# A graph network's edge weights: three BF16 one-hot products replaced by one FP32 product

## The chip, the cores and the metric

The kernel runs on one core of a Trainium2 chip. The metric is device time in microseconds. The time before is the median of three runs.

## The reference

The program is a stack of four graph layers over 3125 nodes with 128 features and 100000 edges, sorted by destination. All four layers use the same edges, so two dense matrices serve them: for each pair of nodes the number of edges between them, and the sum of their edge weights. Only layer 1 reads the second one:

```python
def spmv(v):
    return jax.ops.segment_sum(edge_vals[:, None] * v[edge_col], edge_row, num_segments=n)
...
x = x + _L0_gnn_ref(h, edge_index, ...)              # attention, two rounds: counts
x = x + _L1_gnn_ref(h, edge_weight, weights, src, dst)   # spmv three times: weights
x = x + _L2_gnn_ref(h, src, dst, ...)                # mean over neighbours, three rounds: counts
x = x + _L3_gnn_ref(h, edge_index, edge_type_16, ...)    # messages with edge types
```

## The kernel before

**Nodes, blocks and slots.** The nodes form 25 blocks of 128. A bucket holds the edges from one source block to one destination block; it has a fixed number of slots of 128 edges each. That number, `CAP`, depends on the destination block: 8, 4, 3, 3 for blocks 0 to 3, 2 for blocks 4 to 18 and 1 for blocks 19 to 24. Destination block 0 so has 200 slots, block 1 has 100, blocks 2 and 3 have 76, those with `CAP` 2 have 50 and those with `CAP` 1 have 26.

**Placing the edges (`place_edges`).** Vector, scalar and tensor engine compute the row of each edge in a DRAM table and pack a record of eight BF16 fields per edge into the SBUF tile `rec`: source lane, destination lane, the weight as three BF16 parts whose sum is the FP32 weight (`split3`, lines 919 to 921), and the edge type. Each field is transposed on TensorE (line 1074) and copied from PSUM into `rec` by ScalarE (line 1075). Then 782 indirect DMAs, issued one after the other by GpSimd (POOL, line 1081), scatter 128 records each into the table; each record's row is 64 bytes. The order of these DMAs (`ORDER`) puts the edges of destination blocks 5 to 24 first.

**Building a block (`build_block`).** When the records of a destination block have landed, SyncE loads them (line 1151, one slot to a partition). TensorE transposes every field into the PSUM tile `keys` (line 1157), so that one edge lies on one partition. The slots are then taken in batches of eight. For a batch, VectorE writes two one-hots of 128 x 1024 BF16, `oh_s` and `oh_d` (line 1174), and then `oh_s` times each weight part, three times, into `oh_w` (line 1176). For each slot TensorE computes the counts, `oh_s` by `oh_d` (line 1188), and then three products of `oh_d` with the parts of `oh_w` (line 1191), all in BF16, accumulated over the slots of a bucket in the PSUM tile `ps_cw`. That tile holds two source blocks and has two buffers. ScalarE copies it out: the counts as FP8 into SBUF (line 1195), the weights as FP32 into `w_out` (line 1196), which goes to DRAM from ScalarE's DMA queue (line 1199). At a block's end ScalarE sums the excess of its counts over 15 (line 1201), for a check whose result chooses a general path at the end. The one-hot tiles have two buffers each.

**Order.** `graph_and_layer0` takes the destination blocks in groups: 5 to 8, 9 to 12, 13 to 16, 17 to 20, 21 to 24, then 0 to 2, then 3 and 4. After the blocks of a group have been built, `attend` runs the first attention round for them: per block 25 matmuls with the counts (`ps_u`, line 1331), some of them taken during the build, and then for each of four heads 25 VectorE operations (line 1340), each followed by up to four matmuls (line 1343). The framework's scheduler orders the instructions of each engine when the program is built[...].

Of the kernel before, what the change touches and what calls it, by code (L numbers as in the profile page):

```python
# [18 lines left out]
P = 128  # L19
N = 3125  # L20
NB = 25
# [36 lines left out]
FIELDS = 8  # L58
# [2 lines left out]
ORDER = list(range(LOW[FIRST], ROWS)) + list(range(LOW[FIRST]))  # L61
GROUPS = [(q, q + 4) for q in range(FIRST, NB, 4)] + [(0, 3), (3, 5)]
BATCH = 8
SL, DL, WT, TYPE = 0, 1, 2, 5
CB = [(q, min(4, NB - q)) for q in range(0, NB, 4)]


def bc(ap, shape):
    return ap.to_broadcast(shape)
# [829 lines left out]
class FastGnn(Gnn):  # L899
# [24 lines left out]
    def place_edges(self, placed):  # L924


        nc, tc, a = self.nc, self.tc, self.a
        self.table = self.dram.tile([TABLE, ROOM], BF16, name="table")
        self.types = self.dram.tile([1, EPART * EC], BF16, name="types")
        self.src_of = self.dram.tile([P, EPART, EK], I32, name="src_of")  # L930
        self.dst_of = self.dram.tile([P, EPART, EK], F32, name="dst_of")
# [2 lines left out]
        with ExitStack() as s:  # L934
# [4 lines left out]
            tile = lambda name, dt=F32: work.tile([A, EC], dt, name=name)  # L939


            rec = placed.tile([P, EK * A * FIELDS + ROOM - FIELDS], BF16, name="rec")
            rec_of = rec[:, : EK * A * FIELDS].rearrange("p (k a f) -> p k a f", k=EK, f=FIELDS)
            whole = E // EC
            rest = E - whole * EC
# [3 lines left out]
            for name, dt, fill, skip, queue in loads:  # L949
# [2 lines left out]
                v = a[name[:3] if skip else name]  # L952
                queue.dma_start(t[:whole, :], v[skip : skip + whole * EC].rearrange("(p c) -> p c", c=EC))
                queue.dma_start(t[whole:, : rest - skip], v[whole * EC + skip :][None, :])
            nc.gpsimd.memset(rec, 0.0)
            per = BASE[NB] // P
            none = work.tile([P, 14 * ROOM], BF16, name="none")
            nc.gpsimd.memset(none, -1.0)
            nc.sync.dma_start(self.table[: BASE[NB]].rearrange("(p i r) f -> p i (r f)", p=P, r=14),
                              bc(none[:, None, :], [P, per // 14, 14 * ROOM]))  # L960
            number = tile("number")
            nc.gpsimd.iota(number, pattern=[[1, EC]], base=0, channel_multiplier=EC, allow_small_or_imprecise_dtypes=True)

# [155 lines left out]
    def open_build(self, s, counts):  # L1119
        nc, tc = self.nc, self.tc  # L1120
        self.counts = counts.tile([P, NB, NP], FP8, name="counts8")
        self.weights = self.dram.tile([NB, P, NP], F32, name="weights")
        self.wide = self.dram.tile([2, sum(N_SLOTS[:WIDE]) * P], BF16, name="wide")
        one = self.b_one = s.enter_context(tc.tile_pool(name="build", bufs=1))
        self.b_slots = s.enter_context(tc.tile_pool(name="build_s", bufs=1))
        self.b_hot = s.enter_context(tc.tile_pool(name="build_hot", bufs=2))
        self.b_out = s.enter_context(tc.tile_pool(name="build_out", bufs=3))
        self.b_ps = s.enter_context(tc.tile_pool(name="build_ps", bufs=2, space=PSUM))
        self.b_keys = s.enter_context(tc.tile_pool(name="build_keys", bufs=1, space=PSUM))
        self.lane16 = one.tile([P, P, 2], BF16, name="lane16")  # L1130
        nc.vector.tensor_copy(self.lane16, bc(self.lane[:, :, None], [P, P, 2]))
        self.minus_most = one.tile([P, 1], F32, name="minus_most")
        nc.vector.memset(self.minus_most, -MOST)
        self.above = one.tile([P, NB], F32, name="above")
        self.junk = one.tile([P, NB, P], FP8, name="junk")

    def build_block(self, db):
        nc, tc = self.nc, self.tc
        lane = self.lane16
        cap = CAP[db]  # L1140
        n_slots = N_SLOTS[db]
        halves = -(-n_slots // P)
        rows = n_slots // halves
        need = [self.placed[c] for c in range(LOW[db], ENDS[db])]


        keys = self.b_keys.tile([P, WT + 3, N_SLOTS[0]], BF16, name="keys")
        at = sum(N_SLOTS[:db])
        for a in range(halves):
            r = self.b_slots.tile([P, P, ROOM], BF16, name="slots")  # L1150
            ld = nc.sync.dma_start(r[:rows], self.table[BASE[db] + a * rows * P :][: rows * P].rearrange(
                "(s e) f -> s e f", e=P))
            for ins in need:
                self.wait_for(ld.ins, ins)
            tc.declare_no_dep(ld.ins, group=self.table.tensor.name, keep=need, reason="its edges are in these")
            for f in range(WT + 3):
                nc.tensor.transpose(keys[:, f, a * rows : (a + 1) * rows], r[:rows, :, f], self.ident16[:rows, :rows])
            if db < WIDE:
                rowed = self.b_one.tile([P, 2, P], BF16, name="rowed")
                for i, f in enumerate((SL, TYPE)):  # L1160
                    nc.scalar.copy(rowed[:rows, i], r[:rows, :, f])  # L1161
                    nc.scalar.dma_start(self.wide[i, (at + a * rows) * P : (at + (a + 1) * rows) * P].rearrange(
                        "(s e) -> s e", e=P), rowed[:rows, i])
        if db < WIDE:
            nc.scalar.copy(self.wide_dl[:, at : at + n_slots], keys[:, DL, :n_slots])
        for x0 in range(0, n_slots, BATCH):
            k = min(BATCH, n_slots - x0)
            h = k // 2
            wide = [P, h, P, 2]
            key = lambda f: bc(keys[:, f, x0 : x0 + 2 * h].rearrange("p (a b) -> p a b", b=2)[:, :, None, :], wide)  # L1170
            oh_s, oh_d = (self.b_hot.tile([P, BATCH // 2, P, 2], BF16, name=m) for m in ("oh_s", "oh_d"))
            oh_w = self.b_hot.tile([P, 3, BATCH // 2, P, 2], BF16, name="oh_w")
            for oh, f in ((oh_s, SL), (oh_d, DL)):
                nc.vector.tensor_tensor(oh[:, :h], bc(lane[:, None], wide), key(f), op=OP.is_equal)  # L1174
            for t in range(3):
                nc.vector.tensor_tensor(oh_w[:, t, :h], oh_s[:, :h], key(WT + t), op=OP.mult)  # L1176
            for x in range(k):
                sb, c = divmod(x0 + x, cap)
                if sb == NB:
                    break  # L1180
                i, j = divmod(sb, 2)
                if j == c == 0:
                    ps = self.b_ps.tile([P, 2, 2, P], F32, name="ps_cw")
                if c == 0 and sb % 4 == 0:
                    w_out = self.b_out.tile([P, 4, P], F32, name="w_out")
                of = (slice(None), x // 2, slice(None), x % 2)
                last = c == cap - 1
                nc.tensor.matmul(ps[:, 0, j, :], lhsT=oh_s[of], rhs=oh_d[of], start=(j == c == 0), stop=last,  # L1188
                                 skip_group_check=True)
                for t in range(3):  # L1190
                    nc.tensor.matmul(ps[:, 1, j, :], lhsT=oh_d[of], rhs=oh_w[:, t][of], start=False,  # L1191
                                     stop=(last and t == 2), skip_group_check=True)
                if last and (j == 1 or sb == NB - 1):
                    q, n = 2 * i, j + 1
                    nc.scalar.copy(self.counts[:, q : q + n, db * P : (db + 1) * P], ps[:, 0, :n], saturate=True)  # L1195
                    nc.scalar.copy(w_out[:, q % 4 : q % 4 + n], ps[:, 1, :n])
                    if sb % 4 == 3 or sb == NB - 1:
                        b = sb // 4 * 4
                        nc.scalar.dma_start(self.weights[db, :, b * P : (sb + 1) * P].rearrange("p (b s) -> p b s", s=P),
                                            w_out[:, : sb + 1 - b])  # L1200
        nc.scalar.activation(self.junk, self.counts[:, :, db * P : (db + 1) * P], AF.Relu, bias=self.minus_most,
                             accum_out=self.above[:, db : db + 1], saturate=False)

    def load_graph(self, dst, b, weights=False):
        self.nc.sync.dma_start(dst.rearrange("p b s -> p (b s)"), self.weights[b])
# [705 lines left out]
```

## Time and profile before

| | us |
|---|---|
| Median of the runs | 4530.33 (4530.28 to 4541.58) |
| Profiled execution, its own time | 4554.83 |
| Its span | 4553.0 |
| First and last scatter DMA start (line 1081) | 140.3 and 1207.5 |
| First and last one-hot of the build start (line 1174) | 490.6 and 2225.6 |
| Mean granted TensorE clock | 0.874 |

The profile is of one execution, taken on the chip. Engines are named PE (TensorE matmuls), PEld (its weight loads), DVE (VectorE), ACT (ScalarE), POOL (GpSimd) and SP (SyncE). A row of the groups gives the line of the code, the engine, the operation, the tile written and those read, the shape of one, how many there were, and behind the bar their busy time, the mean of one in ns, and the time for which the engine stood idle just ahead of them with what ended most of it. "remote" stands for a release by something that the profile does not show. A matmul's time in it overlaps with that of the next, so that the distance between two starts tells more than the duration of one. A busy share is an average over stages with different limits.

### The profile page before, as it was taken

How to read it: one execution, taken by the hardware profiler on the slowest of the kernel's cores; microseconds unless marked ns; L12 is line 12 of the kernel's file. 1: busy time of each engine (PE TensorE's matmuls, PEld its weight loads, DVE VectorE, ACT ScalarE, POOL GpSimd, SP SyncE). 2: the span in 40 equal slices, each digit the busy share in tenths (PEclk: the TensorE clock that was granted, in tenths of full speed). 3: DMA queues.
4: the chain of work that ended last, by engine and by line, in shares of the span. 5: the costliest groups of instructions: out<-in, count | busy, mean ns of one | idle time of the engine just before them, and what ended most of it. 6: DMA issues, size and time to landing. Idle time of an engine off the chain costs nothing.

```text
span 4553.0 us, 51360 instructions
## 1 busy us (share of the span) xinstructions
PE 2715.6 (60%) x20811; PEld 1890.9 (42%) x20811; DVE 2399.1 (53%) x3942; ACT 673.3 (15%) x1437; POOL 1277.9 (28%) x1234
## 2 busy tenths in 40 slices
PE   0010000000188878778878885988979994777777
PEld 0010000000156555555545553444455554666666
DVE  8510200000199999899989997011145563444445
ACT  0200100000024313412220001000021111222222
POOL 0577777777400000000000000000012104555553
PEclk9999955555599999999999998999989996888888
DMA  4000000000012101201000001866600003333332
GB/s 131 17 7 6 16 8 8 8 8 12 19 40 73 55 31 55 86 21 40 30 15 1 1 1 60 303 246 235 240 18 1 1 12 99 94 90 98 89 85 68
DMA packets 116937, 276.49 MB, mean 61 GB/s; under 512 B 27445, under 2 KB 67268, under 8 KB 105732
## 3 DMA queue, kind: packets, MB, share of 16 engines
q1 hardware_dynamic: 52182, 198.30, 12.9%
q0 software_dynamic: 37856, 32.76, 3.2%
q10 hardware_dynamic: 26652, 42.05, 2.5%
q8 instruction: 165, 2.70, 0.2%
q14 instruction: 82, 0.67, 0.0%
HBM read 210.00 MB, written 63.02 MB: 60 GB/s over the span
## 4 chain that ended last, share of the span: by engine, by line
PE 33%; DVE 28%; another core or an unknown queue 23%; issue 10%; ACT 4%; DMA 1%; POOL 1%; ACTq 0%; SPq 0%; DVEq 0%; POOLq 0%
DVE over L1340 10%; PE ps_sum L531 9%; DVE oh_w L1176 5%; PE ps_acc L1343 5%; PE agg_wide L1771 3%; PE agg_far L1810 3%; PE ps_agg L1601 3%; PE ps_acc L1331 2%; DVE oh_s L1174 2%; DVE oh_d L1174 2%; PE ps_m L1764 2%; PE ps_cw L1191 1%; PE ps_u L1331 1%; ACT m_wide L1768 1%
## 5 line engine op out<-in xcount | busy, mean ns | idle before, releaser
L1081 POOL DMA_INDIRECT table<-rec,idx x782 | 819.8, 1048 | 379.1 <-issue 248.5
L1343 PE MATMUL ps_acc<-parts,over 128*128 128x198 bf16 x5000 | 622.6, 252 | 166.3 <-DVE over L1340 80.0
L1633 POOL IOTA of_i<- 96x1 int32 x1 | 0.1, 131 | 2119.6 <-PE ps L510 2119.6
L1188 PE MATMUL ps_cw<-oh_d,oh_s 128*128 128x128 bf16 x1350 | 304.7, 228 | 433.2 <-remote 304.4
L1343 PEld LDWEIGHTS <-over 128*128 128x128 bf16 x5000 | 371.5, 98 | 415.3 <-DVE over L1340 392.5
L1789 POOL DMA_INDIRECT m_far<-pre,src x401 | 396.5, 989 | 473.6 <-issue 261.8
L1174 DVE TENSOR_TENSOR oh_s<-lane,keys 128x1024 bf16<-128x1024 bf16 (+2 forms) x187 | 118.3, 633 | 711.5 <-remote 669.7
L1191 PE MATMUL ps_cw<-oh_w,oh_d 128*128 128x128 bf16 x4050 | 400.6, 229 | 94.4 <-DVE oh_w L1176 48.9
L1340 DVE SCALAR_TENSOR_TENSOR over<-ps_row,minus,counts 128x512 bf16<-128x512 f32 (+2 forms) x700 | 424.5, 685 | 4.1 <-ACT rowed L1161 2.2
L531 PE MATMUL ps_sum<-g,v_node 128*128 128x512 f32 (+1 forms) x1050 | 403.7, 547 | 2.2 <-ACT v_node L482 1.4
L1340 DVE SCALAR_TENSOR_TENSOR over<-row,minus,counts 128x640 bf16<-128x640 f32 x500 | 402.0, 878 | 0.6 <-ACT row L1439 0.6
L1191 PEld LDWEIGHTS <-oh_d 128*128 128x128 bf16 x4050 | 313.1, 102 | 133.9 <-issue 112.9
L1188 PEld LDWEIGHTS <-oh_s 128*128 128x128 bf16 x1350 | 136.3, 101 | 464.8 <-issue 401.7
L1176 DVE TENSOR_TENSOR oh_w<-oh_s,keys 128x1024 bf16<-128x1024 bf16 (+2 forms) x561 | 324.9, 631 | 0.0
L1601 PE MATMUL ps_agg<-l_parts,counts 128*128 128x384 bf16 (+1 forms) x1875 | 315.9, 327 | 8.8 <-POOL l_parts L921 8.8
L1331 PE MATMUL ps_u<-parts,counts 128*128 128x396 bf16 x625 | 152.4, 356 | 281.8 <-issue 239.1
L1771 PE MATMUL agg_wide<-m_wide,oh_wide 128*128 128x128 f32 x1100 | 187.8, 322 | 168.2 <-ACT m_wide L1768 105.1
L531 PEld LDWEIGHTS ps_sum<-g,v_node 128*128 128x128 f32 x1050 | 188.0, 190 | 218.0 <-issue 215.2
L1195 ACT ACTIVATE counts<-ps_cw 128x256 fp8e4<-128x256 f32 (+1 forms) x325 | 122.5, 377 | 1021.5 <-remote 731.4
L1331 PEld LDWEIGHTS <-counts 128*128 128x128 fp8e4 x1250 | 112.8, 99 | 384.4 <-issue 302.3
L1601 PEld LDWEIGHTS <-counts 128*128 128x128 fp8e4 x1875 | 183.4, 98 | 133.6 <-issue 10.2
L1771 PEld LDWEIGHTS agg_wide<-m_wide,oh_wide 128*128 128x128 f32 x1100 | 160.7, 224 | 188.0 <-ACT m_wide L1768 122.2
(348 smaller groups left out, 3428.6 us busy)
## 6 DMA issues: line engine op xcount, KB each, us to landing
g<-weights SPq DMA_DIRECT2D x75, 1600.0 KB
weights<-w_out ACTq DMA_DIRECT2D x150, 256.0 KB
src_row<-wide SPq DMA_DIRECT2D x32, 512.0 KB
table<-rec,idx POOLq DMA_INDIRECT x782
type_row<-wide SPq DMA_DIRECT2D x32, 384.0 KB
table<-none SPq DMA_DIRECT2D x1, 10864.0 KB
type_row<-types SPq DMA_DIRECT2D x25, 384.0 KB
m_far<-pre,src POOLq DMA_INDIRECT x401
```

Of the source, the lines that this page charges most:

```text
L531: nc.tensor.matmul(ps[:, c, :w], lhsT=y[:, b, :], rhs=flat[:, c0 : c0 + w], start=(b == 0), stop=(b == NB - 1))
L1081: st = nc.gpsimd.indirect_dma_start(out=self.table, out_offset=bass.IndirectOffsetOnAxis(ap=idx[:, k, p : p + 1], axis=0), in_=rec[:, (k * ...
L1174: nc.vector.tensor_tensor(oh[:, :h], bc(lane[:, None], wide), key(f), op=OP.is_equal)
L1176: nc.vector.tensor_tensor(oh_w[:, t, :h], oh_s[:, :h], key(WT + t), op=OP.mult)
L1188: nc.tensor.matmul(ps[:, 0, j, :], lhsT=oh_s[of], rhs=oh_d[of], start=(j == c == 0), stop=last, skip_group_check=True)
L1191: nc.tensor.matmul(ps[:, 1, j, :], lhsT=oh_d[of], rhs=oh_w[:, t][of], start=False, stop=(last and t == 2), skip_group_check=True)
L1331: nc.tensor.matmul(wide[:, : HEADS * 3 * F1], lhsT=self.counts[:, sb, (a + q) * P : (a + q + 1) * P], rhs=parts[:, sb, :, :, F1:], start=( ...
L1340: V.scalar_tensor_tensor(over[:, : n * P], row, minus[:, sb, i : i + 1], self.counts[:, sb, cols], op0=OP.is_gt, op1=OP.mult)
L1343: nc.tensor.matmul(ps[:, j, : 3 * F2], lhsT=over[:, j * P : (j + 1) * P], rhs=parts[:, sb, i].rearrange("p s f -> p (s f)"), start=(sb == ...
L1601: nc.tensor.matmul(ps[:, :n], lhsT=self.counts[:, sb, db * P : (db + 1) * P], rhs=parts[:, sb, :n], start=(sb == 0), stop=(sb == NB - 1))
L1771: nc.tensor.matmul(agg, lhsT=oh[:, j, :], rhs=m[:, j, :], start=(x == 0), stop=(x == n_slots - 1))
L1789: nc.gpsimd.indirect_dma_start(out=m[:, j, :], out_offset=None, in_=pre, in_offset=bass.IndirectOffsetOnAxis(ap=src_of[:, a + j : a + j + ...
```

## The change

The weight stays one FP32 number. The record keeps its eight 16-bit places; places 2 and 3 hold the FP32 weight, and the edge type moves to place 4. The tile `rec` and the table are declared as 32-bit integers, with the same bytes. In place of three split parts, the raw weight is transposed in FP32 and copied into the record. In the build, one FP32 one-hot `oh_w` (`oh_s` times the FP32 weight) stands for the three BF16 ones, with its elements in order as before; ScalarE copies `oh_d` to FP32 (`oh_d32`), and one FP32 product per slot replaces the three BF16 products. The transposed fields of a block are two in BF16 and one in FP32. The sum over a block's counts is taken in five parts of five source blocks each.

```diff
-SL, DL, WT, TYPE = 0, 1, 2, 5
+SL, DL, WT, TYPE = 0, 1, 2, 4
...
-        self.table = self.dram.tile([TABLE, ROOM], BF16, name="table")
+        self.table = self.dram.tile([TABLE, ROOM // 2], I32, name="table")
...
-            rec = placed.tile([P, EK * A * FIELDS + ROOM - FIELDS], BF16, name="rec")
+            words = placed.tile([P, (EK * A * FIELDS + ROOM - FIELDS) // 2], I32, name="rec")
+            rec = words.bitcast(BF16)
+            rec_w = words[:, : EK * A * FIELDS // 2].bitcast(F32).rearrange("p (k a f) -> p k a f", k=EK, f=FIELDS // 2)
...
-            nc.gpsimd.memset(rec, 0.0)
+            nc.gpsimd.memset(words, 0)
...
-                              bc(none[:, None, :], [P, per // 14, 14 * ROOM]))
+                              bc(none.bitcast(I32)[:, None, :], [P, per // 14, 14 * ROOM // 2]))
...
-            parts = [tile(f"w16_{i}", BF16) for i in range(3)]
-            self.split3(parts, w, tile("rest"), V)
+            for q, n in ((0, 4), (4, EK - 4)):
+                ps = psum2.tile([P, 4, A], F32, name="ps_idx")
+                for j in range(n):
+                    nc.tensor.transpose(ps[:, j, :], w[:, (q + j) * P : (q + j + 1) * P], self.ident[:A, :A])
+                nc.scalar.copy(rec_w[:, q : q + n, :, WT // 2], ps[:, :n])
             of_i = tile("of_i", I32)
-            fields = [(WT + i, p) for i, p in enumerate(parts)]
+            fields = []
...
-                    in_=rec[:, (k * A + p) * FIELDS :][:, :ROOM], in_offset=None)
+                    in_=words[:, (k * A + p) * FIELDS // 2 :][:, : ROOM // 2], in_offset=None)
...
-        self.above = one.tile([P, NB], F32, name="above")
-        self.junk = one.tile([P, NB, P], FP8, name="junk")
+        self.above = one.tile([P, NB * 5], F32, name="above")
+        self.junk = one.tile([P, 5, P], FP8, name="junk")
...
-        keys = self.b_keys.tile([P, WT + 3, N_SLOTS[0]], BF16, name="keys")
+        both = self.b_keys.tile([P, 2, N_SLOTS[0]], F32, name="keys")
+        keys = both[:, 0].bitcast(BF16).rearrange("p (f x) -> p f x", f=2)
+        w_of = both[:, 1]
...
-            for f in range(WT + 3):
-                nc.tensor.transpose(keys[:, f, a * rows : (a + 1) * rows], r[:rows, :, f], self.ident16[:rows, :rows])
+            part = slice(a * rows, (a + 1) * rows)
+            for f in (SL, DL):
+                nc.tensor.transpose(keys[:, f, part], r[:rows, :, f], self.ident16[:rows, :rows])
+            nc.tensor.transpose(w_of[:, part], whole.bitcast(F32)[:rows, :, WT // 2], self.ident[:rows, :rows])
...
-            oh_w = self.b_hot.tile([P, 3, BATCH // 2, P, 2], BF16, name="oh_w")
+            oh_w, oh_d32 = (self.b_hot.tile([P, BATCH // 2, P, 2], F32, name=m) for m in ("oh_w", "oh_d32"))
             for oh, f in ((oh_s, SL), (oh_d, DL)):
-                nc.vector.tensor_tensor(oh[:, :h], bc(lane[:, None], wide), key(f), op=OP.is_equal)
-            for t in range(3):
-                nc.vector.tensor_tensor(oh_w[:, t, :h], oh_s[:, :h], key(WT + t), op=OP.mult)
+                nc.vector.tensor_tensor(oh[:, :h], bc(lane[:, None], wide), key(keys[:, f]), op=OP.is_equal)
+            nc.vector.tensor_tensor(oh_w[:, :h], oh_s[:, :h], key(w_of), op=OP.mult)
+            nc.scalar.copy(oh_d32[:, :h], oh_d[:, :h])
...
-                for t in range(3):
-                    nc.tensor.matmul(ps[:, 1, j, :], lhsT=oh_d[of], rhs=oh_w[:, t][of], start=False,
-                                     stop=(last and t == 2), skip_group_check=True)
+                nc.tensor.matmul(ps[:, 1, j, :], lhsT=oh_d32[of], rhs=oh_w[of], start=False, stop=last,
+                                 skip_group_check=True)
...
-        nc.scalar.activation(self.junk, self.counts[:, :, db * P : (db + 1) * P], AF.Relu, bias=self.minus_most,
-                             accum_out=self.above[:, db : db + 1], saturate=False)
+        for q in range(0, NB, 5):
+            nc.scalar.activation(self.junk, self.counts[:, q : q + 5, db * P : (db + 1) * P], AF.Relu, bias=self.minus_most,
+                                 accum_out=self.above[:, db * 5 + q // 5 : db * 5 + q // 5 + 1], saturate=False)
```

More of the change, by code (lines that the diff above doesn't have):

```diff
@@ L1144, in build_block @@
         need = [self.placed[c] for c in range(LOW[db], ENDS[db])]
-        keys = self.b_keys.tile([P, WT + 3, N_SLOTS[0]], BF16, name="keys")
+        both = self.b_keys.tile([P, 2, N_SLOTS[0]], F32, name="keys")
+        keys = both[:, 0].bitcast(BF16).rearrange("p (f x) -> p f x", f=2)
+        w_of = both[:, 1]
         at = sum(N_SLOTS[:db])
         for a in range(halves):
-            r = self.b_slots.tile([P, P, ROOM], BF16, name="slots")
-            ld = nc.sync.dma_start(r[:rows], self.table[BASE[db] + a * rows * P :][: rows * P].rearrange(
+            whole = self.b_slots.tile([P, P, ROOM // 2], I32, name="slots")
+            r = whole.rearrange("p e f -> p (e f)").bitcast(BF16).rearrange("p (e f) -> p e f", f=ROOM)
+            ld = nc.sync.dma_start(whole[:rows], self.table[BASE[db] + a * rows * P :][: rows * P].rearrange(
                 "(s e) f -> s e f", e=P))
@@ L1169, in build_block @@
             wide = [P, h, P, 2]
-            key = lambda f: bc(keys[:, f, x0 : x0 + 2 * h].rearrange("p (a b) -> p a b", b=2)[:, :, None, :], wide)
+            key = lambda v: bc(v[:, x0 : x0 + 2 * h].rearrange("p (a b) -> p a b", b=2)[:, :, None, :], wide)
             oh_s, oh_d = (self.b_hot.tile([P, BATCH // 2, P, 2], BF16, name=m) for m in ("oh_s", "oh_d"))
-            oh_w = self.b_hot.tile([P, 3, BATCH // 2, P, 2], BF16, name="oh_w")
+            oh_w, oh_d32 = (self.b_hot.tile([P, BATCH // 2, P, 2], F32, name=m) for m in ("oh_w", "oh_d32"))
             for oh, f in ((oh_s, SL), (oh_d, DL)):
-                nc.vector.tensor_tensor(oh[:, :h], bc(lane[:, None], wide), key(f), op=OP.is_equal)
-            for t in range(3):
-                nc.vector.tensor_tensor(oh_w[:, t, :h], oh_s[:, :h], key(WT + t), op=OP.mult)
+                nc.vector.tensor_tensor(oh[:, :h], bc(lane[:, None], wide), key(keys[:, f]), op=OP.is_equal)
+            nc.vector.tensor_tensor(oh_w[:, :h], oh_s[:, :h], key(w_of), op=OP.mult)
+            nc.scalar.copy(oh_d32[:, :h], oh_d[:, :h])
             for x in range(k):
```

## The prediction

> **What bounds the kernel now.** I read four views in this order: the page's engine totals and slices, the instruction groups, the timeline of the graph build, and a table of busy time by stretch. The page first (engine, busy us, share, instructions), then the groups that the change touches:
>
> ```profile
> PE 2715.6 (60%) x20811; PEld 1890.9 (42%) x20811; DVE 2399.1 (53%) x3942; ACT 673.3 (15%) x1437; POOL 1277.9 (28%) x1234
> ...
> L1188 PE MATMUL ps_cw<-oh_d,oh_s 128*128 128x128 bf16 x1350 | 304.7, 228 | 433.2 <-remote 304.4
> ...
> L1191 PE MATMUL ps_cw<-oh_w,oh_d 128*128 128x128 bf16 x4050 | 400.6, 229 | 94.4 <-DVE oh_w L1176 48.9
> ...
> L1176 DVE TENSOR_TENSOR oh_w<-oh_s,keys 128x1024 bf16<-128x1024 bf16 (+2 forms) x561 | 324.9, 631 | 0.0
> ```
>
> No engine is full over the whole span, so the build has to be read by stage. It has two. Until 1236 us POOL scatters edges and the build crawls; the timeline of VectorE there (start, duration, instruction, idle before it):
>
> ```profile
> 558.09 0.69 DVE L1174 TENSOR_TENSOR oh_s<-lane,keys 128x1024 bf16<-128x1024 bf16 x1 [61.39 <-remote]
> 566.49 0.69 DVE L1174 TENSOR_TENSOR oh_d<-lane,keys 128x1024 bf16<-128x1024 bf16 x1 [7.71 <-remote]
> ...
> 656.11 0.69 DVE L1174 TENSOR_TENSOR oh_s<-lane,keys 128x1024 bf16<-128x1024 bf16 x1 [87.15 <-remote]
> ```
>
> With two buffers, oh_s of batch three waits for the last L1188 of batch one and oh_d for the last L1191, three matmuls later on PE: 8.40 us apart, 2.8 us a matmul. That gap returns at 664.51, 768.14, 869.00, 969.82 and 1210.77. From one batch to the next it is 100.8 us (869.00 to 969.82), that is 36 matmuls of 2.8 us: 32 of the eight slots and some four of L1331. So here PE's matmul completions are rationed, whatever their length. FP32 counts double: the two L1258 copies at 393.45 and 404.65 us stand 11.20 us apart, with two FP32 products between, which the trace records as four MATMULs.
>
> After 1236 us the build runs freely, in turns with the attention. Busy time by stretch (stretch, length, then PE, PEld, DVE, ACT, POOL, clock):
>
> ```profile
> 1366.00:1450.00 84.00, 72.67 (x880) 58.25 (x880) 79.60 (x150) 41.56 (x108) 0.00 (x0) 0.95 0.26 90
> 1826.00:1882.00 56.00, 44.17 (x452) 32.39 (x450) 46.28 (x89) 36.77 (x100) 0.00 (x0) 0.91 0.36 121
> 1957.00:2035.00 78.00, 59.48 (x776) 49.96 (x775) 77.97 (x132) 7.97 (x24) 0.00 (x0) 0.91 0.05 18
> 2035.00:2115.00 80.00, 63.46 (x809) 52.21 (x807) 70.44 (x123) 24.52 (x64) 0.00 (x0) 0.91 0.16 59
> ```
>
> The reader is to see DVE at 79.6 of 84 us (blocks 9 to 12, 50 slots each) and 148.4 of 158 us (blocks 0 to 2): VectorE sets the pace. In blocks 21 to 24 (26 slots) nothing is full, but ACT has risen to 36.8 of 56 us.
>
> [...]
>
> **The change part by part.**
>
> *Edge placing.* Two splits and three BF16 fields go; seven FP32 transposes and two PSUM copies come, from raw weights that are there at 39 us, when ACT is idle. POOL starts at 140.26 us, after ACT's last rec copy (128.76 + 10.64 = 139.40) and after idx (138.56). Two of the six rec copies (3.6 us each) leave ACT's final run, which then ends near 132 us; VectorE loses L919 and L921 (1.06 + 1.09), so idx comes at 136.4 and is what is late next: **-3.5 us** (between -2 and -4). All 782 scatters follow POOL's start at their old pace, as each row is 64 bytes still. The integer memset and the table's fill keep their bytes and stand beside 100 us of other work: zero; so do SP's loads of the slots.
>
> *Crawling stage, 496 to 1236 us.* A slot completes 1 + 2 matmuls instead of 4, a batch 8 + 16 + 4 = 28 instead of 36. 740 us then do the work of 740 x 36/28 = 951 old ones: 211/100.8 = 2.1 batches more, each otherwise 3.0 us in the fast stage: **-6 us**. If an FP32 product counts once, 20 per batch, it is 5.9 batches, -18; if transposes or waits take the room, 0.
>
> *VectorE, fast stage.* A batch has 5 one-hot operations 0.60 us apart (1257.01 to 1258.81 holds three), 2.99 us. Now two at 0.60 and one FP32 oh_w[...]. 2.34 us, 0.65 less. The 1158 slots after the first group make 145 batches: 94 us of VectorE time leave.
>
> *TensorE, fast stage.* At full clock L1191's matmuls start 0.057 us apart, so a slot is 0.228. FP32 MATMULs start (4212.52 - 4211.62)/8 = 0.1125 apart, two to a product. A slot becomes 0.057 + 0.225 = 0.28 if the FP32 load hides under a BF16 matmul, 0.33 if it takes its own 0.11; I take 0.305. The product reads every second FP32 element, which no row shows; the BF16 matmuls read with the same step at 0.057, so I take it as free (at worst twice 0.225, which nothing here speaks for; that end stays outside the range). L1331 adds 25 x 0.177 = 4.4 us a block. A 50-slot block: 15.3 + 4.4 = 19.7 us of PE, against 18.7 of DVE before and 14.6 now. **TensorE takes VectorE's place.**
>
> *ScalarE.* [...] A 50-slot block: 13 pairs of evacuations at 0.56 = 7.3, copies 5.9, check 4.0, DMA issues 0.7: 17.9 us; a 26-slot block 15.1, where 11.0 were. The copy stands in order before evacuations; behind those wait PE's two PSUM buffers.
>
> Each stretch's new time is its busiest engine plus the idle that the old busiest one had:
> - blocks 0 to 2 (376 slots): PE 114.7 + 13.3 = 128, + 9.6 = 138 against 158: **-20**
> - blocks 3, 4 (126 slots): PE 38.4 + 8.9, + 4.1 = 51.4 against 57: **-6**
> - blocks 9 to 16 (400 slots): PE 122 + 35.4, + 8.8 = 166 against 169, and 1 us a block for evacuations behind copies: **+5**
> - blocks 17 to 20: ACT 66, + 5.8 = 72 against 69: **+3**
> - blocks 21 to 24: ACT 60.4, less the last check (4) that the attention hides, + about 7 of the old 10 idle = 63 against 56: **+7**
>
> Sum: -3.5 - 6 - 20 - 6 + 5 + 3 + 7 = -20.5 us. The profiled execution took 4554.8 us, so it would be 4534; that execution stands 24.5 us above the median of the three runs, and from 4530.3 the same sum gives **4510 us**. Attention, layers 1 to 3 and the final reduction of 125 columns instead of 25 (0.1 us more) don't move.
>
> **The rivals.**
> - *TensorE keeps up and VectorE's time is all gain.* For it: PE has gaps while DVE is full. At 0.28 a slot and 20 completions a batch: -30, -9, -13, -3, 0, and -3.5 - 18: -76, 4454 us. Against it: the FP32 intervals above.
> - *Slower: the copy sits in ACT's queue.* PE's FP32 product waits for oh_d32, oh_d32 for evacuations before it, and these for PE. In the narrow blocks (98 batches, the first group's rest among them) 0.6 of each 0.95 us copy would show: +56 instead of +15, giving about 4551. Against it: ACT has 2 to 3 us of slack in 20 a block; for it: junk L1201 already held PE 1.47 us at 1847.70. It decides once more than 0.37 us a batch shows, since 36 us of gains stand against it.
> - *A wash:* wide blocks gain 15 and narrow ones lose as much: 4530.
> - *Not what it says:* "one product" is two MATMULs in hardware here. That is in the sum.
>
> **How the numbers follow.** A measurement of this kernel can tell about 0.3% (13.6 us) from no change. Forecast 0.45 (4490 to 4525, a seventh of it inside 0.3%), full gain 0.20, copy queue 0.22, wash 0.13. Faster: 0.45 x 0.85 + 0.20 = 0.58; same: 0.07 + 0.13 = 0.20; slower 0.22. The range reaches from the full gain's point to just past the copy queue's, which leaves out about half of each case, 0.2 in all: 4454 to 4556.
>
> **What would show it.** Right: L1191 becomes x2700 FP32 MATMULs about 0.11 us apart and x1350 products; oh_w x187 at 1.22 us; oh_d32 x187 at 1.04 on ACT; first scatter near 136.7 us; batches 78 us apart until the scatters end; blocks 0 to 2 in some 138 us with PE waiting little for oh_w. Wrong: batches 56 us apart; PE idle before L1191 for ACT's oh_d32, or before L1188 for w_out by over 0.4 us a batch; FP32 pairs over 0.35 us a slot; or a step outside the build that moves.

## The result and the profile after

The changed kernel takes 4604.93 us (median of four runs, 4597.66 to 4612.24) against 4535.95 us for the kernel before beside it: 1.0137 times as long, 95% interval 1.011 to 1.0165, some 69 us more. I had forecast 4510 us and a range up to 4556 us. The profiled execution took 4612.24 us (span 4610.4), against 4554.83 us (span 4553.0) before.

First the page of the kernel after: totals by engine, then the groups of the count product (L1198), of the FP32 product (L1200), of ScalarE's copy (L1186) and of the FP32 one-hot (L1185). The columns after the count are busy time in us, mean ns of one, and idle time before them with what ended most of it.

```profile
PE 2857.4 (62%) x19395; PEld 2042.4 (44%) x19395; DVE 2288.2 (50%) x3566; ACT 856.2 (19%) x1821; POOL 1272.0 (28%) x1234
...
L1198 PE MATMUL ps_cw<-oh_d,oh_s 128*128 128x128 bf16 x1350 | 313.6, 234 | 456.1 <-ACT w_out L1205 230.9
L1200 PE MATMUL ps_cw<-oh_w,oh_d 128*128 128x128 f32 x2700 | 549.6, 333 | 60.2 <-ACT oh_d L1186 38.1
...
L1186 ACT CAST oh_d<-oh_d 128x1024 f32<-128x1024 bf16 (+2 forms) x187 | 178.3, 972 | 393.5 <-DVE oh_d L1184 392.0
L1185 DVE TENSOR_TENSOR oh_w<-oh_s,keys 128x1024 f32<-128x1024 bf16 (+2 forms) x187 | 208.8, 1117 | 60.4 <-remote 55.4
```

VectorE lost 111 us of work (2399.1 to 2288.2), 0.59 us for each of the 187 batches, short ones among them (0.65 was forecast for a full one). TensorE gained 142 us (2715.6 to 2857.4) with fewer instructions. ScalarE gained 183 us and still looks idle at 19%: the total says nothing of the moment at which it is wanted.

The crawling stage first, in VectorE's timeline (start, duration, instruction, idle before it):

```profile
549.13 0.69 DVE L1184 TENSOR_TENSOR oh_s<-lane,keys 128x1024 bf16<-128x1024 bf16 x1 [65.28 <-remote]
...
627.53 0.69 DVE L1184 TENSOR_TENSOR oh_s<-lane,keys 128x1024 bf16<-128x1024 bf16 x1 [70.88 <-remote]
```

A batch takes 78.4 us where it took 100.8, the very number of the forecast (28 completions of 2.8 us). The scatters run from 137.7 to 1202.5 us, where they ran from 140.3 to 1207.5. So the first part of the forecast holds, and the kernel enters the fast stage ahead.

Then busy time by stretch of the fast stage: blocks 9 to 12, blocks 21 to 24 and blocks 0 to 2 (stretch, length, then PE, PEld, DVE, ACT, POOL, clock).

```profile
1354.00:1462.00 108.00, 96.95 (x721) 81.77 (x721) 72.26 (x105) 72.21 (x170) 0.00 (x0) 0.94 0.20 70
1863.00:1942.00 79.00, 66.06 (x454) 51.95 (x454) 46.41 (x74) 61.29 (x162) 0.00 (x0) 0.89 0.29 99
2004.00:2170.00 166.00, 151.04 (x1203) 138.08 (x1202) 121.95 (x160) 85.79 (x162) 0.00 (x0) 0.94 0.10 37
```

The first row is to be held against the 84 us of before: TensorE was busy for 72.67 of them and is now busy for 96.95, with fewer instructions (721 for 880), and VectorE has gone from nearly full to two thirds. TensorE's timeline says why. These are matmuls in the middle of a batch:

```profile
1415.58 0.22 PE L1198 MATMUL ps_cw<-oh_d,oh_s 128*128 128x128 bf16 x1
1415.64 0.45 PE L1200 MATMUL ps_cw<-oh_w,oh_d 128*128 128x128 f32 x2
1415.93 0.22 PE L1198 MATMUL ps_cw<-oh_d,oh_s 128*128 128x128 bf16 x1
1415.99 0.45 PE L1200 MATMUL ps_cw<-oh_w,oh_d 128*128 128x128 f32 x2
1416.28 0.22 PE L1198 MATMUL ps_cw<-oh_d,oh_s 128*128 128x128 bf16 x1
```

From one L1198 to the next is about **0.348 us** (0.347 in the median after 1250 us), a slot's whole time. It was 0.228 and I had taken 0.305. A stretch of four 50-slot blocks has 200 slots, and 200 x 0.120 = 24.0 us. TensorE's busy time has grown by 24.3, but the second window also holds 38 more matmuls of the attention than the first, so that the close agreement is in part chance. The rest of the 108 us is TensorE waiting (who waited for whom, total us, times, longest):

```profile
PE ps_cw L1200 <- ACT oh_d L1186: 6.9, 7, 1.9
PE ps_cw L1200 <- DVE oh_w L1185: 2.8, 1, 2.8
PE ps_cw L1198 <- DVE oh_d L1184: 1.2, 1, 1.2
```

Most of it is for ScalarE's copy, once or twice a block. One of the longest stands at 1411.35 to 1413.26 us. There ScalarE's timeline has the last parts of a block's count check, and the copy behind them at 1412.18 us, though VectorE had written its input `oh_d` by 1410.17 us:

```profile
1410.40 0.83 ACT L1211 ACTIVATE junk<-counts,minus_most 128x640 fp8e4<-128x640 fp8e4 x1
...
1411.35 0.83 ACT L1211 ACTIVATE junk<-counts,minus_most 128x640 fp8e4<-128x640 fp8e4 x1
...
1412.18 1.03 ACT L1186 CAST oh_d<-oh_d 128x1024 f32<-128x1024 bf16 x1
```

Where the time went is read from the ends of the attention stretches (the start of the last VectorE operation of each, L1363 before, L1373 after). The last column is what each stretch adds:

| ends of | before, us | after, us | difference | added |
|---|---|---|---|---|
| blocks 5 to 8 | 1372.77 | 1365.34 | -7.4 | -7.4 |
| 9 to 12 | 1532.52 | 1539.92 | +7.4 | +14.8 |
| 13 to 16 | 1692.29 | 1714.48 | +22.2 | +14.8 |
| 17 to 20 | 1834.32 | 1875.14 | +40.8 | +18.6 |
| 21 to 24 | 1967.04 | 2016.13 | +49.1 | +8.3 |
| 0 to 2 | 2179.19 | 2236.43 | +57.2 | +8.1 |
| 3 and 4 | 2273.78 | 2335.18 | +61.4 | +4.2 |

Afterwards nothing grows: the first matmul of L531 starts 63.9 us later than before, the first of layer 3's wide aggregation (L1771, now L1781) 63.8 us later, and the two spans differ by 57.4 us.

### The profile page after: what moved, and what is told of

Same layout as the page of the kernel before. It is cut to its first block, busy times and chain, and to the rows that moved or that the text cites. A ratio compares the mean times of both kernels' runs of the same rounds, so it can differ in the third digit from the quotient of the medians.

```text
span 4610.4 us, 48788 instructions
## 1 busy us (share of the span) xinstructions
PE 2857.4 (62%) x19395; PEld 2042.4 (44%) x19395; DVE 2288.2 (50%) x3566; ACT 856.2 (19%) x1821; POOL 1272.0 (28%) x1234
## 4 chain that ended last, share of the span: by engine, by line
PE 41%; another core or an unknown queue 23%; DVE 19%; issue 9%; ACT 5%; DMA 1%; POOL 1%; SPq 0%; ACTq 0%; DVEq 0%; POOLq 0%
DVE over L1350 9%; PE ps_sum L531 9%; PE ps_cw L1200 8%; PE ps_acc L1353 5%; PE agg_far L1820 3%; PE agg_wide L1781 3%; PE ps_agg L1611 3%; PE ps_acc L1341 2%; PE ps_cw L1198 2%; PE ps_u L1341 1%; PE ps_m L1774 1%; ACT m_wide L1778 1%; ACT oh_d L1186 1%; ACT junk L1211 1%
## 5 line engine op out<-in xcount | busy, mean ns | idle before, releaser
L1198 PE MATMUL ps_cw<-oh_d,oh_s 128*128 128x128 bf16 x1350 | 313.6, 234 | 456.1 <-ACT w_out L1205 230.9
L1200 PE MATMUL ps_cw<-oh_w,oh_d 128*128 128x128 f32 x2700 | 549.6, 333 | 60.2 <-ACT oh_d L1186 38.1
L1200 PEld LDWEIGHTS ps_cw<-oh_w,oh_d 128*128 128x128 f32 x2700 | 473.3, 219 | 118.7 <-ACT oh_d L1186 53.0
L531 PE MATMUL ps_sum<-g,v_node 128*128 128x512 f32 (+1 forms) x1050 | 403.7, 547 | 2.2 <-ACT v_node L482 2.2
L1198 PEld LDWEIGHTS <-oh_s 128*128 128x128 bf16 x1350 | 143.4, 106 | 465.9 <-remote 250.7
L1341 PE MATMUL ps_u<-parts,counts 128*128 128x396 bf16 x625 | 163.6, 362 | 284.0 <-remote 203.6
L1781 PE MATMUL agg_wide<-m_wide,oh_wide 128*128 128x128 f32 x1100 | 188.3, 323 | 155.9 <-ACT m_wide L1778 110.5
L531 PEld LDWEIGHTS ps_sum<-g,v_node 128*128 128x128 f32 x1050 | 188.0, 190 | 218.0 <-issue 215.2
L1186 ACT CAST oh_d<-oh_d 128x1024 f32<-128x1024 bf16 (+2 forms) x187 | 178.3, 972 | 393.5 <-DVE oh_d L1184 392.0
L1185 DVE TENSOR_TENSOR oh_w<-oh_s,keys 128x1024 f32<-128x1024 bf16 (+2 forms) x187 | 208.8, 1117 | 60.4 <-remote 55.4
```

Of the source, the lines that this page charges most:

```text
L531: nc.tensor.matmul(ps[:, c, :w], lhsT=y[:, b, :], rhs=flat[:, c0 : c0 + w], start=(b == 0), stop=(b == NB - 1))
L1185: nc.vector.tensor_tensor(oh_w[:, :h], oh_s[:, :h], key(w_of), op=OP.mult)
L1186: nc.scalar.copy(oh_d32[:, :h], oh_d[:, :h])
L1200: nc.tensor.matmul(ps[:, 1, j, :], lhsT=oh_d32[of], rhs=oh_w[of], start=False, stop=last, skip_group_check=True)
L1341: nc.tensor.matmul(wide[:, : HEADS * 3 * F1], lhsT=self.counts[:, sb, (a + q) * P : (a + q + 1) * P], rhs=parts[:, sb, :, :, F1:], start=( ...
L1781: nc.tensor.matmul(agg, lhsT=oh[:, j, :], rhs=m[:, j, :], start=(x == 0), stop=(x == n_slots - 1))
```

## The experiments

Three theories. **Theory P:** TensorE's price for a slot is the loss, and it came out above my figure because of the strided read (called S) or of the FP32 weight load (called L). **Theory C:** ScalarE's copy holds the build. **Theory R:** the crawling stage is part of the loss.

The experiments ran on three other chips, and there the crawl does not occur: the kernel before takes 3388.5, 3389.1 and 3387.8 us on them. Each ratio below is against the kernel before on the same chip; times of different runs are set side by side as they are, since those three agree within 1.3 us. Four expectations (both operands and one operand slot after slot, TensorE's price alone, without the count check) were written in the first chip's times, which lie about 1148 us higher (4604.9 for 3456.6 us of the kernel after); their differences are what counts.

**The kernel after, again.** No edit.

> The kernel after, unchanged, beside the kernel before on the chip of the experiments, where the edge table is written without the crawl (the kernel before takes 3388 us there). Theory P: the build's stretches are longer by what TensorE's slot costs, wherever they stand; 1350 slots x (0.348 - 0.228) = 162 us of TensorE's time against what VectorE had as its bound before, so some 60 us over before as in the first comparison: 3440 to 3460 us. Theory R (the crawl was a part of the loss): without it the change is no slower than before: 3370 to 3395 us.

Measured: 3456.55 us, ratio 1.0199 (1.0182 to 1.0216), 67 us more. That is theory P's interval and the same loss as in the first comparison, 69 us: the crawl is not part of it. Theory R falls.

**The kernel before, again.** No edit; for its profile.

> The kernel before, unchanged, for its profile on this chip: 3388 us; slots 0.228 us apart on TensorE, VectorE 2.99 us a batch, stretches of 84 us for four blocks once the edge table is written.

Measured: 3391.42 us (one execution). Here are its scatters, then TensorE's busy tenths in 40 slices of the span and the granted clock, and below them the same two rows of the first trace:

```profile
L1081 POOL DMA_INDIRECT table<-rec,idx x782: 966/972/1907, 140.5 to 1145.6; - x196
```

```profile
PE   0136787878777877788886798898799995889998
...
PEclk9978999999999998999998898998899997999999
```

```profile
PE   0010000000188878778878885988979994777777
...
PEclk9999955555599999999999998999989996888888
```

POOL scatters for 1005 us here and for 1067 in the first trace, but here TensorE is seven to eight tenths busy beside it from slice five on and its clock stays at nine tenths. In the first trace it is nearly idle up to slice eleven, from slice six on at half clock. So the rationed completions come with the chip or its state, not with the program; why, no run here can show. The build's stretches are the same in both places: from the end of blocks 5 to 8 the attention ends lie 159.8, 159.7, 142.0 and 131.4 us apart here and 159.8, 159.8, 142.0 and 132.7 in the first trace.

**Slot after slot in memory.** Both FP32 tiles change their layout:

```diff
-            oh_w, oh_d32 = (self.b_hot.tile([P, BATCH // 2, P, 2], F32, name=m) for m in ("oh_w", "oh_d32"))
+            flat_w = self.b_hot.tile([P, BATCH, P], F32, name="oh_w")
+            oh_w = flat_w.rearrange("p (a b) x -> p a x b", b=2)
+            flat_d = self.b_hot.tile([P, BATCH, P], F32, name="oh_d32")
+            oh_d32 = flat_d.rearrange("p (a b) x -> p a x b", b=2)
...
-                nc.tensor.matmul(ps[:, 1, j, :], lhsT=oh_d32[of], rhs=oh_w[of], start=False, stop=last,
+                nc.tensor.matmul(ps[:, 1, j, :], lhsT=flat_d[:, x], rhs=flat_w[:, x], start=False, stop=last,
```

> Both FP32 one-hots lie slot after slot in memory instead of two slots interleaved; the same instructions otherwise. Theory S (the strided FP32 read is what my sum left out): the slot falls from the 0.348 us of the kernel after to 0.057 + 2 x 0.1125 = 0.282 us, that is 13 us less in a stretch of four blocks and at most 1270 fast slots x 0.066 = 84 us in all, less what the copy and VectorE then keep; time 4520 to 4555 us. Theory L (two FP32 weight loads in a row cost 0.29 us a slot in any layout): slot 0.348, time 4605 +- 8 us. Theory C (the copy in ScalarE's queue holds the build): slot may fall but the waits for the copy grow by as much, time 4585 to 4605 us.

Measured: 3516.01 us, ratio 1.0376 (1.0359 to 1.0394), slower than the kernel after by 59 us and above the intervals of all three theories. TensorE's timeline, and the groups of the two writers:

```profile
523.04 0.22 PE L1201 MATMUL ps_cw<-oh_d,oh_s 128*128 128x128 bf16 x1
523.10 0.44 PE L1203 MATMUL ps_cw<-oh_w,oh_d 128*128 128x128 f32 x2
523.37 0.22 PE L1201 MATMUL ps_cw<-oh_d,oh_s 128*128 128x128 bf16 x1
```

```profile
L1189 ACT CAST oh_d<-oh_d 128x1024 f32<-128x1024 bf16 (+2 forms) x187 | 338.7, 1852 | 385.5 <-DVE oh_d L1187 383.1
L1188 DVE TENSOR_TENSOR oh_w<-oh_s,keys 128x1024 f32<-128x1024 bf16 (+2 forms) x187 | 336.4, 1799 | 0.0
```

The slot falls to 0.333 us only: the stride costs 0.015 of the 0.348, theory S is a small part, and 0.333 is the upper of the two ends that I had named for a product without stride. The layout was paid for elsewhere, since the writers now go through memory with a step of 512 bytes (copy 0.97 to 1.85 us, one-hot 1.12 to 1.80 us in the mean). The run was muddled by that.

**Only the moving operand slot after slot.** The same with `oh_d32` as it was.

> Only the moving operand (the weighted source one-hot) lies slot after slot; the FP32 destination one-hot, TensorE's stationary operand, stays interleaved. If the streaming of the moving operand pays for the stride, this run has all of the gain of the run with both (slot 0.282 us, 4520 to 4555 us). If the loading of the stationary operand pays, it has none (slot 0.348 us, 4605 us). If both pay, the slot is near 0.315 us and the time about half way. Theory L: no gain.

Measured: 3466.65 us, ratio 1.0229 (1.0212 to 1.0246), slot 0.346 us. The moving operand has hardly any of the gain, so that most of the 0.015 us falls to the stationary operand, by subtraction: that one was not run alone. The 10 us over the kernel after go with VectorE's one-hot, which is written with the long step here too (1.80 us in the mean).

**Slot after slot, written in order.**

```diff
-            nc.vector.tensor_tensor(oh_w[:, :h], oh_s[:, :h], key(w_of), op=OP.mult)
-            nc.scalar.copy(oh_d32[:, :h], oh_d[:, :h])
+            nc.vector.tensor_tensor(by_slot(oh_w[:, : 2 * h]), oh_s[:, :h].rearrange("p a x b -> p a b x"), weight, op=OP.mult)
+            nc.scalar.copy(by_slot(oh_d32[:, : 2 * h]), oh_d[:, :h].rearrange("p a x b -> p a b x"))
```

> Both FP32 one-hots slot after slot, as in the run with both, but VectorE and ScalarE write them in the order of memory (their BF16 source is read with a step of two instead). That layout took TensorE's slot from 0.348 to 0.333 us; it lost because its writers went with a step of 512 bytes (1.98 us against 1.22 on VectorE, 1.85 against 0.97 on ScalarE). If the step of the write was what slowed them, VectorE is back at 1.2 to 1.3 us and ScalarE at 1.0 us, and the time is that of after less 5 to 20 us. If it is the step between the two sides, they stay slow and the time stays 50 to 70 us over after.

Measured: 3443.10 us, ratio 1.0162 (1.0143 to 1.0181), 13 us under the kernel after. The writers are back at 1.12 and 0.97 us in the mean, and the slot stays at 0.333. It was the step of the write that had slowed them.

**TensorE's price alone.** Three BF16 products of the plain one-hots in place of the FP32 one; all else as after.

```diff
-                nc.tensor.matmul(ps[:, 1, j, :], lhsT=oh_d32[of], rhs=oh_w[of], start=False, stop=last,
-                                 skip_group_check=True)
+                for t in range(3):
+                    nc.tensor.matmul(ps[:, 1, j, :], lhsT=oh_d[of], rhs=oh_s[of], start=False, stop=(last and t == 2),
+                                     skip_group_check=True)
```

> The kernel after, with its FP32 product replaced on TensorE alone by three BF16 products of the same shape from the plain one-hots (the weights that come out are wrong: they are counts); VectorE still writes the FP32 one-hot and ScalarE still copies. Theory P (TensorE's price is the loss): slot 0.228 us as before, 1270 x 0.12 = 152 us at most less than after, bounded by VectorE's 2.34 us a batch and by ScalarE: 4460 to 4510 us, which is under the kernel before. Theory C (the copy and the cut-up check in ScalarE's queue are the loss): the products no longer wait for the copy, so this run alone does not acquit it, but then the build would still be held by ScalarE's 72 us a stretch: over 4535 us.

Measured: 3351.11 us, ratio 0.9885 (0.9869 to 0.9902); 4460 to 4510 us less 1148 are 3312 to 3362, so theory P's interval is met. With TensorE's old price the rest of the change is a gain of 37 us, and 105 us separate it from the kernel after.

**The same, waiting for the copy.** The three BF16 products take as stationary operand the upper halves of `oh_d32`'s elements:

```diff
-                    nc.tensor.matmul(ps[:, 1, j, :], lhsT=oh_d[of], rhs=oh_s[of], start=False, stop=(last and t == 2),
+                    nc.tensor.matmul(ps[:, 1, j, :], lhsT=half[of + (1,)], rhs=oh_s[of], start=False, stop=(last and t == 2),
```

> The kernel after with three BF16 products in place of the FP32 one, as in the earlier run, but their stationary operand is the upper half of each element of ScalarE's FP32 copy, so they wait for the copy as the FP32 product does (the weights that come out are counts again). The earlier run, which did not wait, took 3351 us. Theory C (the wait for the copy costs by itself): 3380 to 3395 us. Theory P (the wait only matters where TensorE is behind anyway): 3351 to 3362 us.

Measured: 3350.71 us, ratio 0.989 (0.9874 to 0.9907). Here are its TensorE's waits for the copy, and below them those of the kernel after, from its repeat:

```profile
PE ps_cw L1203 <- ACT oh_d L1186: 62.5, 73, 4.1
```

```profile
PE ps_cw L1200 <- ACT oh_d L1186: 42.5, 33, 2.6
```

This run waits longer for the copy than the kernel after does and loses nothing against the run that did not wait: where TensorE has room (busy for 842 of the 1100 us from 200 us on, for 893 in the kernel after), its wait was free. Theory C as a cause by itself falls.

**Without the count check.** The five parts of L1211 are left out, and `above` is set to zero once.

> The kernel after without the count check on ScalarE (its five parts a block are left out, the flag they feed is set to zero). Theory C: the products' waits for the copy, 38 us in all and 7 to 8 us in a stretch of the build, stand behind these 4.0 us a block; without them the time falls by 30 to 40 us to 4565 to 4575 us. Theory P: the waits are partly cover for TensorE's own queue; at most 15 us come back, 4590 to 4605 us.

Measured: 3416.24 us, ratio 1.0078 (1.0061 to 1.0095), 40 us under the kernel after. Against the expectation of theory P (at most 15 us): the wait is not mere cover. Theory C's number is met, but the run before shows that the wait costs only where TensorE is full.

**The check handed out.** A block's five parts are issued one at a time behind the next block's copies:

```diff
             nc.scalar.copy(oh_d32[:, :h], oh_d[:, :h])
+            self.late_check(1)
...
-        for q in range(0, NB, 5):
-            nc.scalar.activation(self.junk, self.counts[:, q : q + 5, db * P : (db + 1) * P], AF.Relu, bias=self.minus_most,
-                                 accum_out=self.above[:, db * 5 + q // 5 : db * 5 + q // 5 + 1], saturate=False)
+        self.late += [(db * 5 + q // 5, self.counts[:, q : q + 5, db * P : (db + 1) * P]) for q in range(0, NB, 5)]
```

> The kernel after, complete, with the five parts of the count check handed out: a block's parts are issued one after each of the next block's batches' copies, instead of all five between two blocks. Leaving the check out took 40 us off (3416 against 3456 us). If it was the burst in ScalarE's queue that held the copy, this run keeps nearly all of that: 3415 to 3425 us. If it was ScalarE's total of work, the time stays at 3445 to 3456 us.

Measured: 3422.13 us, ratio 1.0098 (1.0081 to 1.0115), 34 us under the kernel after with the same work. The wait for the copy has gone from 42.5 to 9.9 us:

```profile
PE ps_cw L1208 <- ACT oh_d L1193: 9.9, 21, 1.0
```

ScalarE's busy time is the same (855.6 and 854.3 us). It was the burst ahead of the copy in ScalarE's queue, not ScalarE's total.

**Products in runs by kind.** All count products of a pair of source blocks in a batch first, then its FP32 products (`slots` holds the batch's slots of one pair):

```diff
+                for x, sb, c in slots:
...
+                    nc.tensor.matmul(ps[:, 0, j, :], lhsT=oh_s[of], rhs=oh_d[of], start=(j == c == 0),
+                                     stop=(c == cap - 1), skip_group_check=True)
+                for x, sb, c in slots:
...
+                    nc.tensor.matmul(ps[:, 1, sb % 2, :], lhsT=oh_d32[of], rhs=oh_w[of], start=False,
+                                     stop=(c == cap - 1), skip_group_check=True)
```

> The kernel after with the products of a pair of source blocks in two runs: first the BF16 count products of its (mostly four) slots in the batch, then their FP32 weight products; the same instructions, another order. Theory L (the FP32 weight load cannot hide under a BF16 product of 0.057 us, so that each change from BF16 to FP32 costs about 0.05 us): one change for four slots instead of four, slot 0.348 down to about 0.30 us; 1350 x 0.045 = 60 us of TensorE's time, of which I expect 30 to 60 us in the kernel's time against after; the wait for the copy falls too, since the counts run ahead of it. If FP32 costs 0.14 us a MATMUL in any order: slot stays at 0.348, only the copy's waits fall, 0 to 15 us.

Measured: 3391.88 us, ratio 1.0009 (1.0003 to 1.0016): 65 of the 67 us are gone with the same instructions, a little over the 30 to 60 expected. The wait for the copy has fallen too, from 42.5 to 24.7 us, so not all of the 65 is the slot's price. TensorE's timeline where a batch has eight slots of one pair:

```profile
1078.28 0.62 PE L1200 MATMUL ps_cw<-oh_d,oh_s 128*128 128x128 bf16 x8
1078.74 2.10 PE L1204 MATMUL ps_cw<-oh_w,oh_d 128*128 128x128 f32 x16
1080.67 0.62 PE L1200 MATMUL ps_cw<-oh_d,oh_s 128*128 128x128 bf16 x8
```

Eight slots in 2.39 us are 0.299 a slot. Within such a run the FP32 MATMULs start 0.118 us apart (medians, here and below); only the step from the first to the second, just behind a BF16 product, is 0.175. In the kernel after every slot has that step: 0.059 us from the BF16 product to the first FP32 MATMUL, 0.171 to the second, 0.117 to the next BF16 product. A change from BF16 to FP32 so costs 0.053 to 0.057 us, about one BF16 product's time, and eight slots have seven changes fewer. The weight loads of the kernel after, beside the matmuls shown above, say where the step comes from:

```profile
1415.59 0.31 PEld L1200 LDWEIGHTS ps_cw<-oh_w,oh_d 128*128 128x128 f32 x2
1415.82 0.10 PEld L1198 LDWEIGHTS <-oh_s 128*128 128x128 bf16 x1
1415.93 0.31 PEld L1200 LDWEIGHTS ps_cw<-oh_w,oh_d 128*128 128x128 f32 x2
```

A slot's first FP32 load starts with the BF16 product, the second 0.115 us later, and the second MATMUL comes behind it; the BF16 product covers only 0.059 us of that. Theory L holds: what the change of type costs is shown by the run; that the second load is the reason is read from the starts of the loads, and no run changes a load alone.

**Both.** Runs by kind, and the check handed out.

> The kernel after with both: products in runs by kind, and the check handed out. The run with the products in runs stands at 3392 us. If the two losses are separate (the change of type on TensorE, the burst ahead of the copy on ScalarE), another 25 to 40 us go: 3352 to 3367 us, faster than before. If the runs by kind had already covered the wait for the copy, at most 10 us go: 3382 to 3392 us.

Measured: 3369.81 us, ratio 0.9949 (0.9932 to 0.9965), 22 us under the runs by kind alone, just short of the 25 to 40 expected, and 52 us under the handed-out check alone. The latter pair waits alike for the copy (12.2 and 9.9 us), so the 52 us are the slot's price by itself: 1350 x 0.049 = 66 us at most.

**All three.** And slot after slot, written in order.

> As the run before it, and the FP32 one-hots slot after slot in memory, written in that order. The layout alone took 13 us off the kernel after (3443 against 3456 us). If TensorE is still the bound, the slot goes from 0.299 to about 0.28 us and 5 to 20 us go: 3340 to 3360 us. If VectorE (2.34 us a batch) or ScalarE is the bound by then, nothing moves.

Measured: 3364.86 us, ratio 0.993 (0.9914 to 0.9947). It is the fastest whole version, below both kernels: 23 us under the kernel before and 92 us under the kernel after. The slot is 0.287 us where a batch has eight of one pair (0.299 without the layout), FP32 MATMULs within a run start 0.112 us apart, and the last step gave 5 us: the foot of the 5 to 20 expected, and a time above 3340 to 3360.

## Why the prediction was wrong

- **Edge placing: near in size, wrong in its path.** First scatter 137.7 us, not 136.7; -2.6 us for -3.5. `idx` was ready at 135.22 us, before my 136.4. But I had set the two new copies of the weight (L1065) at about 39 us. Their first transpose (L1064) waited for `idx` (L1058) and started at 134.83 us, the copies ran from 135.87 to 137.45 us, and the first scatter waited for them. That the two errors nearly cancel is luck.
- **Crawling stage: right where there is one.** Batches 78.4 us apart, and -7.4 us at the end of the first group for the -9.5 of both steps together. On the other three chips there is no such stage, so this term belongs to that chip and not to the change.
- **VectorE: right.** A batch takes 2.33 us (1231.13 to 1233.46) for the 2.34 forecast. The 1.22 us in it for a full FP32 one-hot was an estimate of mine and not read from a run; a full one takes 1.215 us (L1185). Two FP32 operations of the trace before would have given nearly that: 640 elements took 0.82 us (L1223), 512 took 0.68 (L1759), and the line through both puts 1024 at an estimated 1.25.
- **TensorE: the step that failed.** I had named the ends 0.28 and 0.33 us a slot, according to whether the FP32 load hides, and took the middle. Where FP32 and BF16 products alternate it does not hide, to go by the starts of the loads: the second FP32 MATMUL of a slot comes 0.171 us after the first instead of 0.118, and the slot is 0.333 without the stride, 0.348 with it. My 0.1125 us was read in a run of FP32 matmuls one behind the other, and the kernel doesn't have that order. The trace before had shown FP32 loads of 192 ns (L1771) beside BF16 ones of 97 (L1191); with the middle I allowed for half of the difference only. "Taken as free" for the stride was wrong by 0.015 us. The term is 0.043 us a slot too small: 1158 slots x 0.043 = 50 us.
- **ScalarE: the durations were right, the queue was not.** The check takes 101 us over 25 blocks (854.3 less 752.9 us of ScalarE's time, with and without it), 4.06 a block for my 4.0; the copy's mean is 0.97 us, that of a full one 1.05 for my 1.04. Both forecasts were estimates and not read from a run; in the trace before 640 elements took 0.74 us (L1217) and 3200 took 2.87 (L461), and the line through both puts 1024 at an estimated 1.06. But I set the copy beside other work and gave evacuations 1 us a block. Issued as five parts in one piece, the check stands ahead of the next copy, and handing it out gave 34 us. The rival that I priced at 4551 us named that queue, put the decision at 0.37 us a batch and saw it in the narrow blocks. Only 42.5/187 = 0.23 us a batch shows, and it counts in the wide blocks too (7.3 us of it in blocks 9 to 12, 5.0 in blocks 0 to 2): where TensorE is the bound, its wait is lost. Part of the loss comes after the wait. In the kernel after, 109 slots have their two MATMULs 0.32 us apart and take 0.64 us, about half TensorE's rate; with the check handed out they are 55. At 0.29 us each that is an estimated 16 of the 34 us; no run separates it from the wait.
- **The stretches.** Blocks 9 to 16 added 29.6 us for +5, 17 to 20 added 18.6 for +3, 21 to 24 added 8.3 for +7, blocks 0 to 2 added 8.1 for -20, blocks 3 and 4 added 4.2 for -6. "TensorE takes VectorE's place" was right, the height was not. With the two terms as measured my sum is -20.5 + 50 + 34 = +64 us; the trace has +61 at the end of the build and the medians +69. The sum is rough: the 34 us come from another chip, and the 50 us take every slot's extra time as lost.

## What to carry to other kernels

Read a matmul's price from a trace where it has the same neighbours as in the new code: the same FP32 product cost 0.24 us in a run and 0.29 us between BF16 products, and the order alone was worth 65 us of 3457. Before giving work to an engine that is busy for a sixth of the span, look at what stands ahead of it in that engine's queue at the moment it is wanted; here the long step was already cut into five parts, and what helped was to spread them. The wait for the copy was free while TensorE had room and cost some 34 us once TensorE was the bound, so two changes that each look harmless (more work here, a short wait there) have to be priced together.

## What was unexpected in the hardware

- The same program takes 4536 us on one chip and 3388 us on three others. In the two profiled executions (spans 4553.0 and 3389.6 us) 939 us of the difference lie before the first matmul of L531 (2834.7 against 1896.0 us), where TensorE's completions came 2.8 us apart on the one chip while POOL scattered the table, and freely beside the same scatters on the other. Another 226 us lie between the first and the last matmul of L1771 (750.5 against 524.7 us), where POOL gathers by index (L1789). Both are stretches with POOL's indirect transfers; the cause was not found.
- Elementwise writes of FP32 with a step of 512 bytes between neighbours cost ScalarE 1.85 us instead of 0.97 and VectorE 1.80 instead of 1.12 (means over all batches); moving the step to the BF16 reads, where it is 4 bytes, cost neither anything (0.97 and 1.12 us again).
- After some waits TensorE ran at about half rate for a while. In the run with that slow copy it resumed after 2.90 us of idleness, was soon at 0.64 us a slot, and fell back to 0.333 some 3.5 us later. In the kernel after, waits of 1.91 us came out both ways: behind the one that ended at 1413.26 us the slots took 0.35 us; behind the one that ended at 1386.84 us the slots of the first microsecond took 0.35 and those from 1388.85 to 1391.41 us took 0.64. The granted clock was 0.50 in that stretch and 1.00 from 1391.50 to 1395.00 us; behind the other wait, from 1413.26 to 1416.00 us, it was 1.00.
